# Two graph layers for 64 graphs on one core: the first weight turned in eight banks, sums two to an operation, graph 2 turned on TensorE, own orders for the last two graphs and an end in quarters

## The chip, the core and the metric

The kernel runs on one core of one Trainium2 chip, all in fp32. The metric is the device time of one execution in microseconds (us). The kernel before takes 2549.07 us, the median of three runs (2547.32 to 2550.57). The core has five engines with queues of their own: TensorE (PE) for matmuls, VectorE (DVE), ScalarE (ACT), GpSimd (POOL), and SyncE (SP), which here only issues DMA transfers. Each works its queue strictly in order, and semaphores hold an instruction until what it reads is there and what it overwrites is done with. Matmul results land in PSUM, which has eight banks of 128 x 512 fp32; everything else is in SBUF.

## The reference, cut to what matters

There are 64 graphs of 256 nodes with 512 features. `x` is 64 x 256 x 512, `adj` is 64 x 256 x 256.

```python
# layer 0
h = jnp.maximum(_layernorm(x, axis=-1), 0.0)
deg = jnp.sum(adj, axis=-1, keepdims=True)
agg = jnp.einsum('bij,bjf->bif', adj, h) / jnp.maximum(deg, EPS)
x = x + relu(jnp.einsum('bnf,of->bno', jnp.concatenate([h, agg], axis=2), W))
# layer 1
h = jnp.maximum(_layernorm(x, axis=-1), 0.0)
Xw = h @ Wv + bv
sj, si = Xw @ aw[:d, 0], Xw @ aw[d:, 0]
e = leaky_relu(sj[:, None, :] + si[:, :, None] + ab[0], 0.2)
alpha = adj * jnp.exp(e)
transition = alpha / (jnp.sum(alpha, axis=-1, keepdims=True) + 1e-12)
H, Xk = 0, h
for k in range(3):
    H = H + Xk @ Wk[k] + bk[k]
    Xk = jnp.einsum('bij,bjd->bid', transition, Xk)
x = x + relu(H)
```

## The kernel before

**The order is a table.** The kernel records every operation of the whole program in a `Plan`, with the engine it runs on, and what it reads and writes. `plan.stage(name, graph, shift)` opens a stage and sets its base, `graph * TURN + SHIFT`. Every `add(engine, cost, run, reads, writes)` in it gets the number base + `AT[stage][n]`, n counting the operations of the stage. `emit` sorts all operations by that number and hands each engine its queue in that order. The costs passed to `add` go nowhere; the numbers alone decide which operation stands before which. Graphs 0, 1 and 2 have tables of their own (`OWN = 3`, names like `wide_0`), the last four graphs have an extra `SHIFT` for each stage, and the stages `transition` and `moved` of the last two have a table `_late`.

**Start.** `first` loads x of graph 0 in two halves and the four row blocks of W0 into the buffers of x2 to x5. `weights_l0` turns W0 with 32 TensorE transposes (L725), four to a bank, in the banks 1, 2 and 0 in turn; each turned quarter of 128 x 256 is copied by ACT to SBUF (16 copies). `combine0` builds on DVE the 28 sums of quarters that the layer-0 product needs (L740, L742). `weights_l1` turns Wv (L775), forms the two score vectors v = Wv·aw on TensorE from a broadcast copy of aw (`awb`, L768; L785), puts them into `v_sb`, and forms the sums of the weights of layer 1: `lq` on DVE (L804) and `l1` on POOL (L703).

**The stages of a graph.**

- `loads`: x and adj, three graphs ahead.
- `prepare`: `norm_relu` makes h0 (L327 sum, L329 scaling of the sums on POOL, L331 squares, L333 to L335 on POOL, L337 relu), `scaled` makes adj over its row sums. Then both are turned. For graphs 0 and 1, `flip_on_pe` (L373) does it on TensorE with a copy out of PSUM (L379). From graph 2 on, `put` turns 32 x 32 blocks on DVE (L345) and stores them with four transfers from SP to DRAM (L349: `dh<-turned`, `dan<-turneda`), and `get` (L355, in the stage `prepared`) loads them back turned.
- `wide`: h0 times the wide half of W0, as a fast matrix scheme with 26 products instead of 32. 18 sums of 128 x 128 pieces of h (`LEFT_SUMS`, buffer `s`) run on POOL through `pool_op` (L389), for graph 0 on DVE (L387). Products (`P`, L426), copies from PSUM to the buffer `stg` by ACT (`S`, L438), and sums by DVE (L588) alternate in the hand-made order of `STEPS`, or of `EARLY` for graphs 0 and 1, which takes the banks 3 to 6.
- `layer0`: seven products with adj (`main`, L426, its sums at L441), and `finish` (L516), which adds relu of the bank to x.
- `turn1`: the second layernorm to h1, the scores (L613, four DVE operations with an accumulated sum), and `put` of h1.
- `transition`: the scores go to DRAM and come back as a row on all partitions (L624, L625); ACT takes exponentials (L630), DVE the larger of two and the product with adj (L633, L635), ACT the scaling (L641); then it is turned, on TensorE for the early ones.
- `moved`, `once`, `inner`, `turned1`, `outer`: the products of layer 1. `outer` ends with `main`, `finish`, and one transfer of 512 KB to the output (L694).

The engines are joined by few buffers: one `stg` of four pieces, one `p0`, one `q0`, one h0t, banks 0 to 2 for `wide` from graph 2 on and for `layer0`, banks 3 to 5 for `outer`. So the order on each engine decides how the stages of neighbouring graphs overlap.

Of the kernel before, what the change touches and what calls it, by code (L numbers as in the profile page):

```python
# [11 lines left out]
AF = mybir.ActivationFunctionType  # L12
# [13 lines left out]
TURN = 44.55  # L26
AT = {
    "first": (-1017.24, -941.27, -1067.90, -979.42, -1133.31, -1447.98, -1153.03, -1322.56, -861.36, -1000.46, -1271.51, -1112.17, -1031.96,
        -1007.46, -997.64, -1019.48, -995.91, -966.87, -807.55, -710.53, -781.12, -671.89, -691.05, -715.55, -741.64, -649.04, -668.80, -637.21,
        -513.09, -573.30, -611.16, -532.37, -616.22, -652.18, -1057.15, -794.26, -597.00, -1140.64, -889.40, -650.49, -823.54, -717.73, -1031.47,  # L30
        -761.68, -747.99, -593.69, -583.75, -527.52, -656.78, -632.97, -239.87, -431.83, -275.83, -1179.40, -946.09, -433.84, -905.70, -638.56,
        -569.10, -880.53, -782.04, -705.59, -492.83, -421.05, -288.74),
    "inner": (112.00, 118.30, 113.21, 111.00, 119.38, 119.48, 120.51, 123.95, 119.91, 117.78, 125.62, 122.20, 129.97, 123.35, 122.08, 122.94, 143.35),
    "inner_0": (120.04, 124.14, 111.34, 108.02, 121.17, 121.28, 127.27, 128.59, 125.03, 116.12, 137.98, 117.98, 127.36, 129.02, 121.84, 124.49,
        158.46),
    "inner_1": (116.30, 120.49, 114.79, 118.55, 119.44, 121.25, 125.68, 131.77, 125.03, 121.31, 129.70, 128.89, 139.17, 129.13, 123.63, 129.21,
        153.96),
    "inner_2": (117.14, 119.66, 118.60, 112.70, 119.26, 121.13, 124.83, 125.54, 119.49, 118.09, 129.51, 123.19, 123.50, 122.53, 120.98, 119.85,
        132.84),
    "layer0": (8.82, 12.23, 23.66, 30.27, 32.06, 29.03, 34.55, 32.01, 36.75, 34.14, 40.29, 34.61, 40.44, 41.44, 41.62, 36.17, 36.49),  # L40
    "layer0_0": (-200.51, -154.12, -17.22, -72.28, 8.54, -32.05, 23.63, -26.42, 30.82, -16.30, 32.72, -9.73, 34.62, 34.67, 35.87, -8.32, -3.57),
    "layer0_1": (-17.97, 4.41, -34.79, 12.11, 32.36, 15.72, 43.05, 22.64, 44.10, 24.61, 47.37, 27.04, 47.39, 47.89, 48.17, 27.25, 27.35),
    "layer0_2": (16.51, 27.98, 24.87, 29.85, 39.27, 28.73, 40.14, 29.55, 40.49, 31.62, 41.67, 35.42, 41.84, 41.86, 44.64, 35.47, 36.33),
    "loads": (-73.25, -54.78),
    "loads_2": (-570.55, -440.31),
    "moved": (96.10, 94.60, 90.90, 91.65, 92.10, 98.61),
    "moved_0": (74.40, 78.92, 73.46, 86.50),
    "moved_1": (91.74, 94.49, 96.28, 96.47, 101.59, 99.65),
    "moved_2": (92.45, 93.46, 87.17, 93.36, 88.66, 95.64),
    "moved_late": (277.68, 282.26, 301.99, 292.62),  # L50
    "once": (54.49, 60.96, 71.27, 72.69, 100.45, 102.13, 97.01, 101.40, 103.69, 104.26, 107.89, 108.15, 102.72, 101.65, 111.96, 103.21, 108.87,
        104.14, 109.67, 110.05, 110.23),
    "once_0": (61.39, 68.65, 43.72, 76.81, 102.31, 108.28, 88.12, 81.94, 109.93, 110.01, 111.86, 113.88, 100.99, 87.31, 97.51, 91.16, 118.80, 101.72,
        103.42, 103.65, 107.11),
    "once_1": (66.98, 69.71, 84.14, 73.11, 100.43, 102.58, 97.12, 100.84, 104.63, 106.78, 110.21, 112.55, 110.97, 102.83, 112.58, 108.30, 112.06,
        106.52, 108.00, 110.24, 114.90),
    "once_2": (48.31, 85.20, 76.99, 85.55, 99.90, 100.10, 96.57, 97.65, 102.25, 103.85, 102.31, 107.68, 98.75, 105.26, 111.34, 111.29, 114.34,
        108.24, 109.43, 112.02, 115.28),
    "outer": (110.55, 112.56, 124.59, 130.71, 122.70, 126.64, 130.05, 124.51, 132.31, 132.69, 134.42, 130.55, 136.29, 137.75, 137.79, 134.66, 140.16,
        142.97, 144.27, 143.30, 141.14, 144.88, 147.05, 147.31, 154.75, 166.76, 149.89, 152.90, 180.04, 173.32, 178.81, 183.03),  # L60
    "outer_0": (75.64, 100.62, 136.69, 136.53, 104.98, 130.05, 133.80, 126.65, 135.71, 136.92, 137.86, 135.82, 139.47, 140.60, 141.14, 138.11,
        143.83, 144.28, 144.84, 145.15, 143.50, 148.77, 148.79, 152.22, 164.19, 164.74, 149.82, 155.17, 176.64, 177.49, 176.45, 180.92),
    "outer_1": (116.86, 117.84, 128.53, 124.70, 122.55, 133.39, 134.11, 129.95, 135.65, 136.44, 136.94, 134.18, 139.81, 139.88, 141.12, 136.84,
        143.12, 148.89, 149.66, 146.81, 143.91, 148.56, 149.77, 153.75, 159.49, 159.72, 152.49, 156.26, 164.38, 167.52, 171.63, 187.33),
    "outer_2": (109.82, 117.34, 125.19, 132.21, 122.42, 127.44, 130.36, 123.94, 131.81, 132.14, 134.85, 131.51, 136.29, 138.25, 138.62, 135.11,
        140.08, 141.11, 142.64, 144.31, 139.88, 144.08, 146.43, 149.56, 150.02, 152.80, 151.35, 151.79, 159.27, 158.56, 152.70, 181.89),
    "prepare": (-58.85, -58.04, -62.77, -50.47, -50.61, -50.10, -47.67, -44.00, -35.79, -33.31, -40.71, -40.92, -34.53, -30.46, -9.67, -12.00,
        -30.84, -30.59, -19.83, -17.85, -13.42, -16.63, -13.01, -0.86, -2.11, 0.02, -0.84),
    "prepare_0": (-1266.53, -975.17, -811.01, -687.47, -880.33, -683.51, -631.06, -581.34, -621.45, -471.77, -1128.62, -1029.34, -1034.44, -882.61,
        -476.14, -489.14, -495.72, -471.07, -383.05, -399.08),  # L70
    "prepare_1": (-557.96, -458.29, -573.61, -253.06, -248.24, -448.75, -390.09, -379.42, -209.99, -190.33, -642.97, -325.85, -355.58, -242.70,
        -180.44, -173.98, -131.68, -163.72, -123.16, -162.03),
    "prepare_2": (-239.11, -208.13, -283.36, -178.85, -105.45, -128.88, -95.37, -80.24, -60.94, -70.06, -131.95, -63.34, -57.66, -46.88, -50.72,
        -47.06, -39.69, -38.58, -74.39, -50.57, -47.70, -74.26, -35.20, -31.13, -44.27, -36.41, -25.44),
    "prepared": (-10.65, 2.40, -0.87),
    "prepared_0": (-266.03, -448.40, -238.28, -282.28),
    "prepared_1": (-42.49, -39.69, 9.83, -23.75),
    "prepared_2": (-15.15, -0.37, 11.90),
    "transition": (55.63, 60.89, 66.16, 59.33, 66.37, 62.85, 61.19, 61.54, 61.61, 62.29, 62.78, 69.44, 69.86, 65.50, 84.98, 85.82, 78.93, 86.06),
    "transition_0": (-37.87, -34.45, 59.61, 61.95, 59.61, 59.97, 69.12, 70.02, 69.57, 70.91, 71.09, 73.37, 74.08, 94.36, 73.26, 95.01, 76.83),  # L80
    "transition_1": (41.14, 59.01, 60.68, 59.69, 61.21, 66.18, 58.69, 58.69, 58.88, 60.76, 61.81, 69.31, 69.66, 62.81, 83.27, 81.85, 79.74, 81.08),
    "transition_2": (48.98, 68.97, 59.08, 59.45, 64.06, 66.35, 59.35, 61.89, 61.81, 62.34, 62.37, 69.62, 73.39, 66.89, 81.35, 84.81, 82.67, 86.91),
    "transition_late": (-54.45, -49.51, 1.31, -11.56, 5.58, 1.28, 1.86, 18.81, 4.03, 18.88, 19.04, 24.08, 44.52, 30.73, 24.06, 60.74, 64.88),
    "turn1": (34.41, 40.31, 39.20, 37.21, 37.30, 39.30, 43.54, 44.94, 46.57, 47.03, 54.64, 55.20, 55.64, 56.82, 51.30, 51.88, 64.71, 63.98, 58.81,
        56.74),
    "turn1_0": (-37.13, -10.01, -7.88, -26.00, -25.40, -17.44, 11.38, 11.78, 24.35, 28.13, 30.44, 32.22, 43.73, 49.19, 23.26, 23.32, -152.13, -56.73,
        -93.40, -120.59),
    "turn1_1": (23.38, 31.87, 33.04, 29.38, 31.30, 34.45, 39.81, 41.29, 33.66, 34.98, 42.54, 47.50, 58.19, 58.12, 39.23, 35.62, 58.55, 66.38, 62.43,
        46.18),
    "turn1_2": (38.62, 40.24, 40.52, 41.94, 43.04, 43.41, 41.83, 46.90, 48.66, 49.26, 50.41, 54.34, 53.15, 56.69, 48.74, 51.03, 53.76, 56.22, 66.90,  # L90
        64.83),
    "turned1": (112.10,),
    "turned1_0": (76.53,),
    "turned1_1": (120.50,),
# [33 lines left out]


LEFT_SUMS = (  # L130
    (8, '-', 3, 7), (9, '+', 1, 8), (10, '+', 2, 8), (11, '-', 5, 9), (12, '-', 0, 4), (13, '-', 6, 12),
    (14, '-', 2, 13), (15, '+', 1, 3), (16, '+', 4, 6), (17, '+', 16, 15), (18, '-', 5, 12), (19, '-', 1, 18),
    (20, '+', 4, 5), (21, '+', 7, 16), (22, '+', 2, 3), (23, '+', 22, 20), (24, '+', 0, 22), (25, '-', 6, 10),
)
# [764 lines left out]
```

## Time and profile before

| | us |
|---|---|
| median of 3 runs | 2549.07 (2547.32 to 2550.57) |
| the profiled execution | 2546.46 |
| its span, first to last instruction | 2544.7 |
| TensorE busy | 2505.8 |
| VectorE busy | 1677.1 |
| ScalarE busy | 1317.8 |
| GpSimd busy | 1688.7 |
| first product of `wide` for graph 0 starts | 24.96 |
| last matmul ends | 2539.95 |

The profile gives, for one execution, the busy time of each engine, the chain of work that ended last, the groups of equal instructions with what ended the idle time ahead of them (`<-`), and the issues of the DMA queues with their time to landing. A line like `L426 PE MATMUL bank<-l,s 128x256 x3292 | 877.4, 380` names line, engine, operation, output and inputs, shape, count, busy time in us and mean ns of one. Matmuls are pipelined, so the mean of one holds its latency, and two in a row take less than twice that. These groups matter for the change:

| group | count | busy us, mean ns |
|---|---|---|
| L725 PE, transposes of W0 | 32 | 7.9, 427 |
| L775 PE, transposes of Wv | 16 | 3.4, 387 |
| L373 PE, flips of h0 | 8 | 1.7, 354 |
| L389 POOL, `s<-h0t,s`, sums of h, 128x128 | 620 | 313.2, 514 |
| L389 POOL, `s<-h0t`, sums of h, 128x128 | 372 | 199.3, 551 |
| L389 POOL, `s<-s,h1t`, sums of 128x256 | 189 | 140.9, 746 |
| L438 ACT, `stg<-bank` | 958 | 342.8, 372 |
| L329 POOL, `sm<-sm` | 128 | 29.5, 230 |
| L349 SP, `dh<-turned`, 128 KB, to landing | 504 | 3.3 us |
| L355 SP, `h0t<-dh`, 512 KB, to landing | 62 | 4.2 us |
| L694 SP, `out_dram<-x`, 512 KB, to landing | 64 | 3.1 us |

### The profile page before, as it was taken

How to read it: one execution, taken by the hardware profiler on the slowest of the kernel's cores; microseconds unless marked ns; L12 is line 12 of the kernel's file. 1: busy time of each engine (PE TensorE's matmuls, PEld its weight loads, DVE VectorE, ACT ScalarE, POOL GpSimd, SP SyncE). 2: the span in 40 equal slices, each digit the busy share in tenths (PEclk: the TensorE clock that was granted, in tenths of full speed). 3: DMA queues.
4: the chain of work that ended last, by engine and by line, in shares of the span. 5: the costliest groups of instructions: out<-in, count | busy, mean ns of one | idle time of the engine just before them, and what ended most of it. 6: DMA issues, size and time to landing. Idle time of an engine off the chain costs nothing.

```text
span 2544.7 us, 40786 instructions
## 1 busy us (share of the span) xinstructions
PE 2505.8 (98%) x12414; PEld 2211.5 (87%) x12414; DVE 1677.1 (66%) x4179; ACT 1317.8 (52%) x3490; POOL 1688.7 (66%) x3162
## 2 busy tenths in 40 slices
PE   7899999999999999999999999999999999999998
PEld 5688888888888888888888888888888888888886
DVE  5777666666666666666666666666666666666653
ACT  6555555555555555555555555555555555555521
POOL 3557766667667677667667667667666676676653
PEclk9999999999999999999999999999999999999999
DMA  4454454454454454454554554544544544545421
GB/s 137 113 128 121 114 126 118 117 128 113 115 135 113 114 127 118 119 121 115 128 121 112 128 123 112 128 119 118 125 113 119 132 112 115 133 109 121 114 67 44
DMA packets 576912, 297.95 MB, mean 117 GB/s; under 512 B 419251, under 2 KB 542899, under 8 KB 576694
## 3 DMA queue, kind: packets, MB, share of 16 engines
q1 hardware_dynamic: 576694, 295.35, 47.7%
q8 instruction: 99, 1.62, 0.3%
q14 instruction: 119, 0.97, 0.2%
HBM read 163.33 MB, written 131.92 MB: 116 GB/s over the span
## 4 chain that ended last, share of the span: by engine, by line
PE 95%; DMA 1%; DVE 1%; issue 1%; ACT 0%; POOL 0%; SPq 0%; DVEq 0%; POOLq 0%; ACTq 0%
PE bank L426 95%; DMA h0t<-dh 0%; DMA l<-in_L_gnn_Wv_dram 0%; DMA dh<-turned 0%; DMA x<-in_x_dram 0%; ACT stg L438 0%; POOL hf L389 0%; SPq L314 0%; DVE x L516 0%; POOL s L389 0%; DVE turned L345 0%; PE bank L775 0%; DVE z L613 0%; PE bank L373 0%; DVE stg L588 0%
## 5 line engine op out<-in xcount | busy, mean ns | idle before, releaser
L426 PE MATMUL bank<-l,s 128*128 128x256 f32 x3292 | 877.4, 380 | 6.8 <-DVE bank L441 2.9
L426 PEld LDWEIGHTS bank<-l,s 128*128 128x128 f32 x3292 | 609.2, 190 | 93.2 <-POOL s L389 3.9
L438 ACT COPY stg<-bank 128x256 f32<-128x256 f32 x958 | 342.8, 372 | 508.7 <-PE bank L426 188.2
L426 PE MATMUL bank<-l,zg 128*128 128x256 f32 x1820 | 468.1, 380 | 3.6 <-POOL zg L389 1.5
L426 PE MATMUL bank<-lq,zg 128*128 128x256 f32 x1792 | 448.2, 379 | 1.2 <-DVE zg L441 0.9
L426 PEld LDWEIGHTS bank<-lq,zg 128*128 128x128 f32 x1792 | 339.8, 190 | 49.5 <-DVE zg L441 1.5
L426 PEld LDWEIGHTS bank<-l,zg 128*128 128x128 f32 x1820 | 336.2, 190 | 45.7 <-POOL zg L389 1.7
L389 POOL TENSOR_TENSOR zg<-zg 128x256 f32<-128x256 f32 (+1 forms) x187 | 133.7, 728 | 355.2 <-ACT zg L438 343.3
L588 DVE TENSOR_TENSOR bank<-bank,stg 128x256 f32<-128x256 f32 x514 | 214.4, 428 | 213.5 <-PE bank L426 146.5
L389 POOL TENSOR_TENSOR s<-h0t,s 128x128 f32<-128x128 f32 x620 | 313.2, 514 | 0.0
L426 PE MATMUL bank<-l,h0t 128*128 128x256 f32 x1008 | 289.5, 380 | 2.1 <-DVE q L588 1.1
L426 PEld LDWEIGHTS bank<-l,h0t 128*128 128x128 f32 x1008 | 197.3, 196 | 25.1 <-DVE q L588 1.5
L613 DVE SCALAR_TENSOR_TENSOR z<-h1n,v_sb 128x512 f32<-128x512 f32 x256 | 200.0, 781 | 11.0 <-ACT h1n L337 2.7
L389 POOL TENSOR_TENSOR s<-h0t 128x128 f32<-128x128 f32 x372 | 199.3, 551 | 7.2 <-DMA h0t<-dh 7.2
L426 PE MATMUL bank<-l,h1t 128*128 128x256 f32 x784 | 202.1, 379 | 1.8 <-DVE lo L444 1.8
L438 ACT COPY qf<-bank 128x256 f32<-128x256 f32 x128 | 47.6, 372 | 291.1 <-DVE qf L441 258.7
L331 ACT ACTIVATE h1n<-x,sm 128x512 f32<-128x512 f32 x130 | 92.9, 715 | 158.9 <-POOL sm L329 158.9
L516 DVE SCALAR_TENSOR_TENSOR x<-bank,x 128x512 f32<-128x512 f32 x256 | 166.4, 686 | 10.4 <-PE bank L426 9.7
L426 PEld LDWEIGHTS bank<-l,h1t 128*128 128x128 f32 x784 | 152.8, 196 | 19.4 <-DVE lo L444 2.6
L329 POOL TENSOR_SCALAR sm<-sm 128x2 f32<-128x2 f32 x128 | 29.5, 230 | 197.6 <-DVE x L516 138.9
L426 PE MATMUL bank<-q,sa 128*128 128x256 f32 x512 | 153.6, 382 | 2.7 <-DVE bank L441 2.0
L389 POOL TENSOR_TENSOR qf<-qf 128x256 f32<-128x256 f32 x124 | 90.9, 733 | 98.2 <-DVE qf L441 98.2
(170 smaller groups left out, 4584.5 us busy)
## 6 DMA issues: line engine op xcount, KB each, us to landing
dh<-turned SPq DMA_DIRECT2D x504, 128.0 KB, 3.3
h1t<-dh SPq DMA_DIRECT2D x64, 512.0 KB, 3.9
out_dram<-x SPq DMA_DIRECT2D x64, 512.0 KB, 3.1
x<-in_x_dram SPq DMA_DIRECT2D x63, 512.0 KB, 4.6
h0t<-dh SPq DMA_DIRECT2D x62, 512.0 KB, 4.2
a<-in_adj_dram SPq DMA_DIRECT2D x64, 256.0 KB, 4.4
dan<-turneda SPq DMA_DIRECT2D x248, 64.0 KB, 1.9
raw<-dan SPq DMA_DIRECT2D x62, 256.0 KB, 2.7
```

Source lines behind the costliest of these rows:

```text
L329: add("POOL", 0.23, lambda: nc.gpsimd.tensor_scalar(sm, sm, -1.0 / F, None, op0=ALU.mult), [], parts(smk))
L331: add("ACT", 0.9, lambda c=c: nc.scalar.activation(h[:, c, :], s[:, c, :], AF.Square, bias=sm[:, c : c + 1], accum_out=sq[:, c : c + 1]), ...
L389: add("POOL", cost, lambda: getattr(nc.gpsimd, f)(to, p, q), reads, [write])
L426: nc.tensor.matmul(ps, lhs, rhs, start=start, stop=True, skip_group_check=True)
L438: add("ACT", 0.37, lambda: nc.scalar.copy(dst, bank[b][:, cols]), [f"bank{b}"], dkeys)
L516: add("DVE", 0.75 if sums else 0.69, lambda c=c: nc.vector.scalar_tensor_tensor(t[:, c, :], bank[banks[1 + c]], 0.0, t[:, c, :], op0=ALU.m ...
L588: add("DVE", 0.43, lambda f=f, to=to, x=x, y=y: getattr(nc.vector, f)(to, x, y), pbk + [k], tok)
L613: add("DVE", 0.83, lambda s=s, c=c: nc.vector.scalar_tensor_tensor(scr.rearrange("p c n -> p (c n)"), h[:, c, :], 1.0, v_sb[:, s, :], op0= ...
```

## The change

1. **W0.** The 32 transposes go to all eight banks in a new order. Seven of the sixteen quarters (`IN_PSUM`) are no longer copied; the DVE sums read them from PSUM. 15 of the 28 sums have such an operand. `combine0` is now part of `weights_l0`.
2. **Sums of h.** The 18 sums of `wide` are made by 9 operations of 128 x 256, two sums each (`pair` builds the access pattern with a stride between the two pieces, or a broadcast of one). `LEFT_SUMS` and `LEFT` are new. They run on POOL for graph 0 too; only its three sums in `q0` stay on DVE.
3. **Small moves.** The scaling of the sums in `norm_relu` goes from POOL to ACT. The four `lq` sums go from DVE to POOL.
4. **Graph 2.** Its h0 is turned on TensorE in the banks 0 and 1, with a copy by ACT, instead of `put` and `get`. Its scaled adj still goes through DRAM.
5. **Graph 1.** `wide(1)` uses the buffers `MZ` and half of `lo5` in place of `stg`; `layer0(1)` uses the banks 3, 4 and 5.
6. **Score vectors.** aw is used as a weight of two columns: 4 matmuls to 2 x 512 instead of 8 to 128 x 512, 4 one-column ones instead of 8, then two matmuls with `sel` (two partitions, 512 columns) and a small one spread the result to all partitions. The broadcast copy of aw is gone.
7. **The last two graphs** have tables of their own for every stage (`_late`, `_last`), and their sums in `zg`, `qf`, `st` and `hf` run on DVE.
8. **The last output.** For graph 63 `main` gets two more banks and `last`: each quarter of the result (128 x 256) is added to x by its own DVE operation and sent by its own transfer of 128 KB.
9. **All numbers** of `AT`, `SHIFT` and `TURN` (44.55 to 38.01) are new, so the order of every engine's queue changes.

```diff
-TURN = 44.55
+TURN = 38.01
...
+IN_PSUM = (27, 29, 31, 33, 35, 36, 37)
...
-        add("POOL", 0.23, lambda: nc.gpsimd.tensor_scalar(sm, sm, -1.0 / F, None, op0=ALU.mult), [], parts(smk))
+        add("ACT", 0.22, lambda: nc.scalar.mul(sm, sm, -1.0 / F), [], parts(smk))
...
     def pool_op(f, cost, to, p, q, reads, write):
-        if plan.graph < 2 and write[:2] in ("zg", "qf", "st") and plan.name[:4] != "wide" or plan.graph == 0:
+        writes = write if isinstance(write, list) else [write]
+        if plan.graph < 2 and writes[0][:2] in ("zg", "qf", "st") and plan.name[:4] != "wide" or plan.graph == 0 and writes[0][:2] == "q0" or (
+                plan.graph >= G - 2 and writes[0][:2] in ("zg", "qf", "st", "hf")):
...
-    def main(terms, banks, seeds, keys, fifth):
+    def main(terms, banks, seeds, keys, fifth, last=None):
...
+        if last:
+            x, y = banks[3:]
+            plus(bank[x][:, lo], [f"bank{x}"], p, lo, s21[:, 1], keys[1:])
+            last(1, hi, x, lo)
+            plus(bank[d][:, lo], [f"bank{d}"], p, lo, s21[:, 0], keys[:1])
+            step(2, r, lo, terms)
+            add("ACT", 0.37, lambda: nc.scalar.copy(bank[y][:, lo], bank[r][:, hi]), [f"bank{r}"], [f"bank{y}"])
+            last(0, lo, r, lo)
+            step(3, y, lo, terms)
+            last(0, hi, y, lo)
+            step(4, d, lo, terms)
+            last(1, lo, d, lo)
+            return
...
     def prepare(g):
...
+        if g < 3:
+            flip_on_pe(h, F, tr_banks if g < 2 else itertools.cycle((0, 1)), H0T[0] if g != 1 else H1T[0])
+        else:
+            put(h, F, TURNED[0], of(D["h0"], g))
         if g < 2:
             early[g] = an
-            flip_on_pe(h, F, tr_banks, H0T[0] if g == 0 else H1T[0])
         else:
-            put(h, F, TURNED[0], of(D["h0"], g))
             put(an, N, of(TURNED_A, next(turns)), of(D["an"], g))
...
-        for i, (to, op, a, b) in enumerate(LEFT_SUMS):
-            pool_op("tensor_add" if op == "+" else "tensor_sub", 0.47, sums[i][0], left[a][0], left[b][0], left[a][1] + left[b][1], sums[i][1])
-            left[to] = sums[i][0], [sums[i][1]]
+        def pair(a, b):
+
+            (x, xk), (y, yk) = left[a], left[b]
+            if a == b:
+                return x.unsqueeze(1).to_broadcast([P, 2, P]), xk
+            step = y.offset - x.offset
+            return bass.AP(tensor=x.tensor, offset=x.offset, ap=[list(x.ap[0]), [step, 2], list(x.ap[-1])]), xk + yk
+
+        for both, op, a, b in LEFT_SUMS:
+            for j in both:
+                to, key = sums(j - 8)
+                left[j] = to, [key]
+            (to, keys), (x, xk), (y, yk) = pair(*both), pair(*a), pair(*b)
+            pool_op("tensor_add" if op == "+" else "tensor_sub", 0.8, to, x, y, xk + yk, keys)
         stage = [(st[:, i], f"{stk}.{i}") for i in range(4)]
+        if g == 1:
+            stage = [(MZ[0][0][:, i], f"{MZ[0][1]}.{i}") for i in range(3)] + [(lo5[:, 1], "lo5.1")]
...
-        (p0, pk), banks = P0[0], (0, 1, 2)
+        (p0, pk), banks = P0[0], (0, 1, 2) if g != 1 else (3, 4, 5)
...
+        def last(c, cols, b, at):
+            part = t[:, c, cols], f"{k}.{c}{cols.start}"
+            add("DVE", 0.43, lambda: nc.vector.scalar_tensor_tensor(part[0], bank[b][:, at], 0.0, part[0], op0=ALU.max, op1=ALU.add),
+                [f"bank{b}", f"{k}.{c}"], [part[1]])
+            add("SP", 0.4, lambda: nc.sync.dma_start(out[g, c * P : (c + 1) * P, cols], part[0]), [part[1]], [f"out{g}.{part[1]}"], 2.2)
...
-        for n in (0, 2, 1, 3):
-            for kk in range(0, FC, 2):
-                b = next(banks)
...
+        for n, kk, b in ((0, 0, 0), (0, 2, 1), (2, 0, 6), (2, 2, 5), (1, 0, 2), (1, 2, 4), (3, 2, 3), (3, 0, 7)):
...
+                if f in IN_PSUM:
+                    assert sign > 0
+                    ps[f] = bank[b][:, cols], f"bank{b}"
...
+        def product(b=b):
+            for oc in range(FC):
+                matmul(bank[b][:2, :], awc[:, :, oc], wvt[oc][0], oc == 0)
...
         for s in range(2):
             b = next(banks)
-
-            def product(b=b, s=s):
-                for oc in range(FC):
-                    matmul(bank[b], awb[:, s, oc, :], wvt[oc][0], oc == 0)
-            add("PE", 3.45, product, awbk + [f"wvt{oc}" for oc in range(FC)] + wvt[0][1] + wvt[2][1], [f"bank{b}"])
+            add("PE", 0.9, lambda b=b, s=s: matmul(bank[b], sel[:, s], vrow[:, :F], True), vrk + ["sel"] + zk, [f"bank{b}"])
...
-            add("DVE", 0.97, lambda to=to, f=f, p=p, q=q: getattr(nc.vector, f)(WQF[to], p, q), pk + qk, [f"lq_{to}"], port=True)
+            add("POOL", 1.3, lambda to=to, f=f, p=p, q=q: getattr(nc.gpsimd, f)(WQF[to], p, q), pk + qk, [f"lq_{to}"], port=True)
...
-                kind = name + (f"_{g}" if g < OWN else "_late" if g >= G - 2 and name in ("transition", "moved") else "")
+                kind = name + (f"_{g}" if g < OWN else "_last" if g == G - 1 else "_late" if g == G - 2 else "")
```

## The prediction

> **What bounds the kernel now.** I began with the shares and the slices of the span, to see whether one engine bounds it.
>
> ```profile
> span 2544.7 us, 40786 instructions
> PE 2505.8 (98%) x12414; PEld 2211.5 (87%) x12414; DVE 1677.1 (66%) x4179; ACT 1317.8 (52%) x3490; POOL 1688.7 (66%) x3162
> PE   7899999999999999999999999999999999999998
> ```
>
> TensorE is busy 98%; only the first two slices and the last are not full. The chain of waits says how unbroken the middle is, and what held the opening.
>
> ```profile
> 75.37 5.71 DMA h0t<-dh
> ...
> 105.46 3.97 DMA h0t<-dh
> ...
> 115.86 1038.04 PE bank L426 x5172
> 1153.99 1275.86 PE bank L426 x6356
> ```
>
> From 115.86 to 2429.85 the chain is matmuls alone. So I cut the span there, and read each engine's busy time (and its instructions) by stretch; the first number after the comma is the length.
>
> ```profile
> 0.00:24.96 24.96, 12.04 (x52) 9.92 (x53) 7.53 (x23) 14.56 (x42) 4.17 (x14) 0.87 0.99 324
> 24.96:48.79 23.83, 23.62 (x106) 16.05 (x106) 16.89 (x49) 17.68 (x45) 7.72 (x10) 0.99 0.08 26
> 48.79:81.59 32.80, 24.24 (x95) 16.68 (x94) 28.18 (x73) 16.92 (x47) 17.99 (x33) 0.95 0.39 95
> 81.59:115.86 34.27, 28.24 (x135) 22.28 (x133) 26.32 (x69) 20.42 (x57) 20.58 (x44) 1.00 0.49 102
> 115.86:2429.85 2313.99, 2313.90 (x11529) 2059.24 (x11530) 1549.47 (x3852) 1222.73 (x3236) 1589.95 (x2982) 1.00 0.50 120
> 2429.85:2484.25 54.40, 53.63 (x274) 46.80 (x274) 26.45 (x64) 15.70 (x40) 29.20 (x53) 1.00 0.24 57
> 2484.25:2509.87 25.62, 22.90 (x101) 18.59 (x100) 13.80 (x34) 7.21 (x17) 10.86 (x16) 1.00 0.22 54
> 2509.87:2539.95 30.08, 27.27 (x131) 21.93 (x129) 7.60 (x17) 2.61 (x7) 8.23 (x13) 1.00 0.08 29
> ```
>
> The middle runs at 2313.99 / 11529 = 200.7 ns an instruction. Busy time overstates a starved stretch, since a matmul that follows a gap shows its whole latency; so I price each stretch by 200.7 ns times its instructions. Lost are: 12.9 us before 24.96 (24.96 − 12.04); nothing to 48.79; 32.80 − 95 × 0.2007 = 13.7; 34.27 − 135 × 0.2007 = 7.2; 110.10 − 506 × 0.2007 = 8.5 from 2429.85 to 2539.95; and 2544.70 − 2539.95 = 4.8 after the last matmul. Together 47 us. That is the ceiling of any change that leaves the matmuls as they are, and all of it lies in the first 116 us and the last 115.
>
> **Start to the first product, 12.9 us lost.** The rows that matter later stand here once:
>
> ```profile
> 21.49 2.82 PE L775 MATMUL bank<-ident,l 128*128 128x128 f32 x12 [5.11 <-DMA l<-in_L_gnn_Wv_dram]
> 24.11 1.06 PE L373 MATMUL bank<-ident,h0n 128*128 128x128 f32 x4
> ...
> 45.81 2.36 POOL L703 TENSOR_TENSOR l<-l,l 128x1024 f32<-128x1024 f32 x1
> 46.30 2.16 DVE L387 TENSOR_TENSOR q<-q 128x256 f32<-128x256 f32 x1
> ...
> 2539.50 1.29 DVE L516 SCALAR_TENSOR_TENSOR x<-bank,x 128x512 f32<-128x512 f32 x2 [4.48 <-PE bank L426]
> 2540.82 0.38 SPq L694 DMA_DIRECT2D out_dram<-x  x1
> ```
>
> Graph 0's second flip stands on TensorE behind twelve Wv transposes, which wait 5.11 us for their load. In the new order the Wv transposes stand behind both flips, among wide(0). What remains ahead is 32 W0 transposes (2.79 + 1.11 + 4.10), which still end near 14.85 since the last W0 load released them at 10.75, and two flips. The first flip needs the ACT relu that began at 14.86 (flip at 15.72); the second relu (18.18 before, behind five other ACT operations) is now next in ACT's queue, so it runs about 15.7 to 16.5, the flip to 17.1. wide(0) starts at 17.1 to 18.5; I take 17.7. TensorE's work ahead of it is 12.04 − 2.82 + 0.5 = 9.7, so 8.0 is lost. Of the 16 W0 copies (0.37 each) 7 go, their quarters being read from PSUM by 15 of the 28 sums (0.42 each, PSUM or not, as the rows `bank<-bank,stg` 428 ns and `l<-zg` 418 ns show), so ACT loses 2.6 us here.
> Against it: graph 0's 18 sums of h leave DVE (18 × 0.29 = 5.2) for POOL, in 9 pairs of 0.75 to 0.84 (rows `s<-s,h1t` 746 and `s<-h1t` 842) = 7.2 us, and matmuls wait for them one by one. I take 1.5 lost (bounds 0.5 to 5; the upper one if DVE and POOL hinder each other as at 46.30, where a sum took 2.16 beside POOL's 2.36 instead of 0.42). Loss 9.5 against 12.9: gain 3.4 (0 to 5).
> [...]
>
> **48.79 to 81.59, 13.7 lost.** Before, one chain of graph 0 goes through it: x0 done 57.12, statistics, h1n 61.97, two transposes 1.39, scores to 66.46, the store of the scores, which SP issues at 65.59, 1.6 after the first two scores (63.95), behind four h transfers, the row at 69.36, exponentials 73.27, product 77.29, `an` 78.5, flips 79.96 and 81.34, first use 84.12: 27 us. The other work that could fill it, wide(2), waits for its h0t, issued at 75.37 and 5.71 on the way. After: graph 2's h is turned on TensorE (8 × 0.11 = 0.9 us more PE work, eight DMA issues and the round trip gone), wide(1) writes its intermediate products to MZ and layer0(1) uses banks 3 to 5, so that wide(2), some 19.5 us of matmuls, can run between them. On the chain itself go 1.4 (the transposes now stand behind the first scores), that 1.6 of SP's queue (the row's two issues now precede all four h transfers), 0.4 (sm on ACT: 0.22 for POOL's 0.23, without the crossing of engines) and 1.4 (the second copy of the flips, which waited on ACT from 81.4 to 82.84): 27 to 22 us, against some 20 us of work placed ahead of its end. Loss 4 or so. **81.59 to 115.86, 7.2 lost:** its head is graph 3's h0t (issued 105.46, 3.97 in flight) and gaps at POOL's sums. The round trip stays, but pair sums cut POOL from 9.3 to 7.2 us a graph; I take 4. Together 20.9 to 8: gain 12.9. Bounds: 4, if wide(2)'s DVE and ACT hand-offs stall it as often as they stall this stretch now (nine waits, 8.5 us, over half of them behind DVE), and 17, if only the 4 us excess of the chain is left.
>
> **PE work.** The v product takes 4 matmuls of 512 columns instead of 8 (8 × 0.44 = 3.5, so 1.75 off) and 4 + 1 one-column ones instead of 8 (0.11 each, 0.35 off); two `sel` matmuls add 0.9 and the flips 0.9. Net −0.3: called 0 (−1 to 0.5). Its chain is longer by two ACT copies (0.6, 0.3); v is first needed by graph 0's scores near 62, so it is hidden; uncovered it costs 1 us.
>
> **The middle, 2314 us.** Work per graph on TensorE is the same. POOL falls by some 2 us a graph, ACT rises by 0.22 × 2, both below two thirds busy. All the queues are reordered, but TensorE works in pairs of 0.43 us and in both orders the closest hand-offs leave one pair for a DVE operation of 0.42. So nothing, the cover being TensorE's own queue. If the cover fails by 0.1 us a graph, 6 us.
>
> **The end, 8.5 + 4.8 lost.** The last tail was 1.29 of DVE (after PE) and 3.9 of SP and DMA. In quarters it is one 128x256 operation (0.43), then a 128 KB transfer: 64 KB rows (`dan`) land in 1.9 and 512 KB in 3.1, so 2.0 to 2.9. Tail 4.8 to 3.1: gain 1.7; it needs one more ACT copy (0.37), ahead of the end. Own orders for graphs 62 and 63, and DVE (0.43) for POOL (0.73) in their sums, shorten hand-offs: five at `bank L441`, 2.9 us, two at `lo L444`, 1.8. I take 8.5 to 6.9, 1.6. Gain 3.3 (0.5 to 7).
> [...]
>
> **Sum.** 3.4 + 12.9 + 0 + 0 + 3.3 = 19.6, nearly all of it at the opening. The profiled execution took 2546.46 (span 2544.7 and 1.8 around it), 2.6 below the median of 2549.07, which runs from 2547.32 to 2550.57. Against the median, 2549.07 − 19.6 = 2529.5; called 2529.
>
> **Rivals.**
> *The middle breaks* (the other side). One hand-off a graph, such as a POOL sum of a reordered queue or a scaling on ACT that now stands behind a copy, comes late. Each 0.1 us is 6 us over 60 graphs; the gain of 20 is gone at 0.33 us a graph, and from 0.42 the change is slower by 5. At 0.5 (somewhat more than one pair) it is 2529 + 30 = 2559. For it: every number of the order is new, and POOL (69%) and DVE (67%) in the middle are not idle enough to catch up at once. Against: the row of the middle has 0.09 us of idle in 2314, the work is the same or less on POOL, and distances are alike.
> *The opening stays bound.* wide(2) starts early but shares DVE with wide(1) (DVE is already 28.18 of 32.80 busy in that stretch) and the sums on POOL; what is not lost waiting for h0t is lost at DVE. Then the two stretches give 4, the start 1, the end 3.3: 2549 − 8 = 2541. For it, that 86%; against, DVE stands there behind SBUF sums that POOL stretches fivefold, as at 46.30, and the four `lq` sums (0.7 each) leave it.
> *The transfer is only swapped:* graph 3's round trip becomes the head and takes back the 4 us given to it: 2533, inside my range.
> *The change does not do what it says:* wide(2) still waits for a buffer of wide(1), and start and end alone count: 2549 − 6.7 = 2542.
>
> **How the numbers follow.** Forecast, gain of 13 to 27: 0.62. Opening bound or wide(2) still waiting, 2537 to 2544: 0.22 together. Middle broken: 0.16, half of it beyond the point where it is slower. Two executions of this kernel differ by up to 0.13%, so 0.2% (5.1 us) is about what can be told from no change. Faster 0.62 + 0.20 and 0.03 of the broken middle = 0.85, same 0.07, slower 0.08. The range goes from 2519 (bounds 5 + 17 + 7 + 1 = 30 of gain) to 2545 (a gain of 4).
>
> **What would show it.** Right: the first L426 row at 17 to 18.5; no wait for `h0t<-dh` of graph 2 and fewer than 10 us lost from 48 to the unbroken chain, which then begins about 16 us earlier for the same work; last DVE operation of 0.43 and four out transfers, the tail near 3. Wrong: gaps between 120 and 2400, which the chain would show as many short pieces behind DVE or POOL; DVE operations of 1 to 2 us beside POOL ones before 40.

## The result, and the profile after

The changed kernel takes 2596.07 us (median of 6 runs, 2594.43 to 2597.35) against 2548.38 for the kernel before (median of 6): ratio 1.0186, 95% interval 1.0173 to 1.0199. It is slower by 47.7 us, where 20 us less were forecast. The profiled execution took 2595.58, its span 2593.6.

The page of the changed kernel: span, busy engines, and the engines' shares of the chain that ended last.

```profile
span 2593.6 us, 39696 instructions
PE 2520.8 (97%) x12412; PEld 2207.0 (85%) x12412; DVE 1720.0 (66%) x4172; ACT 1325.7 (51%) x3616; POOL 1526.0 (59%) x2466
PE 59%; DMA 14%; ACT 13%; POOL 7%; DVE 5%; issue 2%; SPq 0%; POOLq 0%; DVEq 0%; ACTq 0%
```

The shares of the kernel before:

```profile
PE 95%; DMA 1%; DVE 1%; issue 1%; ACT 0%; POOL 0%; SPq 0%; DVEq 0%; POOLq 0%; ACTq 0%
```

TensorE is still busy 97%, and that one per cent says little: its share of the chain has fallen from 95% to 59%. DMA, ACT and POOL hold a third of it. The same work by stretch, cut where the unbroken chains of before have their counterparts (length after the comma, then busy time and instructions):

```profile
0.00:108.95 108.95, 82.96 (x368) 60.10 (x369) 70.44 (x172) 70.47 (x196) 61.05 (x92) 0.97 0.45 126
108.95:2400.69 2291.74, 2257.36 (x11167) 1993.48 (x11168) 1542.08 (x3734) 1193.19 (x3256) 1394.12 (x2263) 1.00 0.47 118
2400.69:2590.01 189.32, 180.50 (x878) 153.47 (x877) 107.10 (x267) 62.08 (x164) 70.82 (x113) 1.00 0.29 70
2590.01:2593.60 3.59, 0.00 (x0) 0.00 (x0) 0.42 (x1) 0.00 (x0) 0.00 (x0) 0.79 0.44 146
```

At 200.7 ns an instruction the losses are as follows, before and after. Each stretch is counted in one piece; a matmul that lies across a cut counts on both sides, so the prediction's shorter stretches add up to 388 and 506 matmuls where there are 383 and 504.

| | before | after |
|---|---|---|
| opening | 115.86 − 383 × 0.2007 = 39.0 | 108.95 − 368 × 0.2007 = 35.1 |
| middle | 0.1 | 2291.74 − 11167 × 0.2007 = 50.5 |
| end, to the last matmul | 110.10 − 504 × 0.2007 = 8.9 | 189.32 − 878 × 0.2007 = 13.1 |
| after the last matmul | 4.8 | 3.6 |

So the middle, unbroken before, loses 50 us; the opening gains 4, and the end loses some 3 net. Nearly all of TensorE's waiting in the middle has one name (total, times, longest):

```profile
PE bank L463 <- ACT tt L396: 33.9, 55, 1.2
```

Once a graph it waits 0.6 us for ACT's copy of the turned transition, `tt`; the first product of `once` reads it. With the restart that is some 0.8 a graph: in the turn shown below, the four matmuls ahead of the gap and the four behind it take 1.58 and 0.55 us from start to start, where the same eight take 0.86 and 0.44 in the kernel before. The chain of waits shows what closes on itself; here is one turn of it, the columns being start, length and what.

```profile
1231.02 22.41 PE bank L463 x116
...
1253.87 1.23 DVE x L567 x4
...
1260.63 1.51 ACT h1n L372 x2
...
1263.12 0.56 ACT ant L396
...
1263.69 5.96 DMA raw<-dtt
...
1269.67 0.66 ACT tt L396
...
1270.37 22.41 PE bank L463 x116
```

From one `once` to the next is 1270.37 − 1231.02 = 39.35 us, against the 38.5 of TensorE's own work (the turn of the first experiment below, where nothing waits). It is a ring, a chain of waits that closes on itself, so that its length sets the time of a graph: 22.41 us of matmuls end layer 0 of graph g; its x, its statistics and its relu follow; then ACT copies graph g+1's scaled adj out of `raw` to `ant`, which has nothing to do with x, but stands behind the relu in ACT's queue. Only then is the single buffer `raw` free for the load of graph g−1's transition, which takes 5.96 us, and `once` of g−1 waits for it. The kernel before has the same ring, but its load is faster. This is the load's row in the two kernels, before and after (count, size, median us to landing):

```profile
raw<-dtt SPq DMA_DIRECT2D x61, 256.0 KB, 3.0
raw<-dtt SPq DMA_DIRECT2D x61, 256.0 KB, 5.9
```

What differs around it is seen on SP's queue, first in the kernel before, then after:

```profile
1277.79 0.36 SPq L355 DMA_DIRECT2D raw<-dtt  x1
1280.11 0.34 SPq L624 DMA_DIRECT2D ds<-sj  x1
```

```profile
1263.01 0.34 SPq L692 DMA_DIRECT2D ds<-sj  x1
1263.69 0.36 SPq L390 DMA_DIRECT2D raw<-dtt  x1
```

The store of the scores (`ds`, 1 KB) used to follow the load by 2.3 us; now it goes 0.7 ahead of it. In the tables the two stand 50.84 and 50.97 (relative to graph g): 0.13 apart.

### The profile page after: what moved, and what is told of

Its sections match the earlier page's. It is cut to its first block, busy times and chain, and to the rows that moved or that the text cites. A ratio compares the mean times of both kernels' runs of the same rounds, so it can differ in the third digit from the quotient of the medians.

```text
span 2593.6 us, 39696 instructions
## 1 busy us (share of the span) xinstructions
PE 2520.8 (97%) x12412; PEld 2207.0 (85%) x12412; DVE 1720.0 (66%) x4172; ACT 1325.7 (51%) x3616; POOL 1526.0 (59%) x2466
## 4 chain that ended last, share of the span: by engine, by line
PE 59%; DMA 14%; ACT 13%; POOL 7%; DVE 5%; issue 2%; SPq 0%; POOLq 0%; DVEq 0%; ACTq 0%
PE bank L463 59%; DMA raw<-dtt 13%; ACT h1n L372 3%; ACT h1n L366 3%; POOL s L426 3%; POOL rstd L369 3%; DVE x L567 2%; ACT tt L396 1%; ACT stg L475 1%; ACT ant L396 1%; ACT an L574 1%; DVE qf L478 1%; ACT bank L649 1%; ACT sm L364 0%; POOL nmr L370 0%
## 5 line engine op out<-in xcount | busy, mean ns | idle before, releaser
L463 PE MATMUL bank<-l,s 128*128 128x256 f32 x3292 | 887.9, 380 | 4.7 <-DVE bank L478 2.5
L463 PE MATMUL bank<-lq,zg 128*128 128x256 f32 x1792 | 438.9, 380 | 4.0 <-DVE mz L478 2.9
L426 POOL TENSOR_TENSOR st<-tt 128x128 f32<-128x128 f32 x120 | 54.8, 456 | 326.2 <-ACT tt L396 326.2
L426 POOL TENSOR_TENSOR q<-q 128x256 f32<-128x256 f32 x189 | 166.8, 895 | 117.6 <-DVE q L656 117.6
L426 POOL TENSOR_TENSOR s<-h0t,s 128x256 f32<-128x256 f32 x315 | 230.9, 741 | 0.7
L364 ACT ACTIVATE sm<-sm 128x2 f32<-128x2 f32 x128 | 26.1, 204 | 333.6 <-DVE x L567 331.7
L681 DVE SCALAR_TENSOR_TENSOR z<-h1n,v_sb 128x512 f32<-128x512 f32 x256 | 177.3, 692 | 20.3 <-ACT h1n L372 13.6
L426 POOL TENSOR_TENSOR zg<-zg 128x256 f32<-128x256 f32 x180 | 141.0, 783 | 79.2 <-DVE zg L478 59.5
L426 POOL TENSOR_TENSOR sa<-ant 128x128 f32<-128x128 f32 x128 | 59.2, 462 | 183.6 <-ACT ant L396 183.6
L426 POOL TENSOR_TENSOR s<-h0t 128x256 f32<-128x256 f32 x189 | 143.4, 772 | 19.3 <-ACT h0t L414 8.9
```

The costliest lines, as they stand in the source:

```text
L364: add("ACT", 0.22, lambda: nc.scalar.mul(sm, sm, -1.0 / F), [], parts(smk))
L426: add("POOL", cost, lambda: getattr(nc.gpsimd, f)(to, p, q), reads, writes)
L463: nc.tensor.matmul(ps, lhs, rhs, start=start, stop=True, skip_group_check=True)
L681: add("DVE", 0.79, lambda s=s, c=c: nc.vector.scalar_tensor_tensor(scr.rearrange("p c n -> p (c n)"), h[:, c, :], 1.0, v_sb[:, s, :], op0= ...
```

## The experiments

All edits are to the changed kernel unless said otherwise. The numbers of the tables are relative to a graph's base, and where an edit holds for some graphs only, the new numbers stand in a table of their own for these.

**The ring cut at both strands.** For graphs 5 to 57 the copy to `ant` goes ahead of the relu, the load ahead of the store.

```diff
-    "prepared": (-13.22, 3.34, 8.63),
+    "prepared": (-13.22, 3.34, 4.49),
-    "moved": (88.98, 92.24, ...),
+    "moved": (87.51, 92.24, ...),
```

> Theory (a ring): graph g's x leads through its relu on ACT to the copy of `raw` to `ant`, which stands behind that relu; only then is `raw` free for the load of `dtt`, and the first product of `once` waits for that. With the copy ahead of the relu, and the load ahead of the scores' store on SP, for graphs 5 to 57, the ring is cut: the first product of `once` no longer waits, a graph takes 38.5 us instead of 39.4, and the time falls by about 53 x 0.83 = 44 us, to some 2552. Rival (the queues as a whole are too tight): the wait moves to another hand-off of DVE, POOL or ACT, and less than half of the 44 us comes back: above 2574.

Measured 2550.47 (before beside it 2548.01): 45.6 us less. The load lands in 2.7, and the chain is matmuls alone from 243.16 to 2279.9:

```profile
243.16 2036.74 PE bank L465 x10148
```

In that stretch the wait moved nowhere else. (Whether a second buffer for `raw` would do the same was not tried.)

**Only the copy to `ant`.**

> Only the copy of `raw` to `ant` goes ahead of the relu; the load of `dtt` still stands behind the store of the scores on SP, which issues at 1263.01 where the load issued at 1263.69. Theory (a ring, with two strands of nearly one length): the load moves by 0.3 us only, so some 53 x 0.33 = 17 us come back, about 2579. If the copy alone were the cause, all 44 would come back (2552); if it had no part, nothing (2596).

Measured 2587.87: 8.2 us less, half of what was expected, and far from 44. The load still goes 0.43 behind the store and lands in 6.1.

**Only the load ahead of the store.**

> Only the load of `dtt` goes ahead of the store of the scores on SP. Theory: it still waits for the copy at 1263.67, so nothing comes back (2596); the store of the scores is 0.7 us later, which costs nothing if the row has room. If SP's queue alone were the cause, 44 us would come back (2552).

Measured 2556.84 (one run): 39 us less, where nothing was expected. My theory of two strands of one length was wrong. The load is still issued when the copy behind the relu frees the buffer, 0.4 us ahead of the store; but its median landing is 2.8, and that alone makes the ring shorter than TensorE's work. TensorE waits for `tt` 8 times instead of 55. So the copy behind the relu is a part of the ring, but not what made it too long. The order has a price for the other side: the store, now 0.4 us behind the load, lands in a median of 5.2 us (3.8 in the changed kernel, 3.0 in the first experiment).

**What else is in flight moved away.** For graphs 5 to 57 the first h1 store and the load of x, issued 2 us behind the slow load, go behind the row.

```diff
-    "turn1": (..., 58.21, 56.06, 54.36, 57.84),
-    "loads": (-58.38, -36.44),
+    "turn1": (..., 58.21, 56.06, 56.00, 57.84),
+    "loads": (-50.00, -36.44),
```

> The order of raw, `ant` and the scores stays; the first of the four h1 stores and the load of x, which SP issues 2 us behind the load of `dtt`, go behind the row. Theory of a collision of transfers: the load of `dtt` then takes about 3 us, as in the kernel before, instead of 5.9; the ring is then 39.4 - 2.9 = 36.5 us, shorter than the 38.5 of TensorE's work, and about 44 us come back (2552) though nothing else is changed. If the 5.9 us have another cause, the landing time stays and so does the time (2596).

Measured 2654.53: 58 us slower. As a test of the time it missed, since the edit made a ring of its own: x, behind stores that wait, now comes just when graph g+3's statistics need it (the chain has 9.8% of `x<-in_x_dram`). But the landing answers the question: 5.4 us, with x 18 us and the h1 store 3.3 us behind the load, when a load of 3 us would have landed. So these two were not what made it slow.

**The store moved away instead.** The scores' store goes behind the first h1 store and x; the load keeps its place and its neighbours.

```diff
-    "transition": (50.84, 55.74, ...),
+    "transition": (55.70, 55.74, ...),
```

> In the changed kernel the store of the scores (1 KB) moves behind the first h1 store and the load of x on SP, for graphs 5 to 57; `ant` and the load of `dtt` keep their places, so that load is still issued when the copy behind the relu frees `raw`. Theory (the load of `dtt` is slow since it is issued 0.4 to 0.7 us behind the store of the scores): it lands in about 2.8 us instead of 5.9 with the h1 store and x still behind it, the ring is 39.4 - 3.0 = 36.4 us, and the time falls to some 2552. Rival (it is slow by sharing with the h1 store and x): the landing stays near 5.9 and the time near 2596. If both count, in between.

Measured 2641.66, again a miss in time for a reason of its own: the scores, their row and the softmax are late, and the chain now has 15% of `ds<-sj` in a window of 60 us (9% over the whole execution). The landing is 2.7, with the h1 store 2.1 and x 2.5 us behind the load, as before the edit. Together the two runs settle it: the load is slow with the store close ahead of it, and not by the bigger transfers behind it.

**The kernel before, with the load put behind the store.** One number changed, for graphs 5 to 57.

```diff
-    "moved": (96.10, 94.60, ...),
+    "moved": (100.20, 94.60, ...),
```

> The kernel before with one number changed: for graphs 5 to 57 the load of `dtt` goes right behind the store of the scores on SP, as in the changed kernel. In its profile the load is issued at 1277.79 and lands in 3.0, the store is issued at 1280.11, and between the copy `tt` and the first product of `once` there are 2.2 us of slack. Theory (the load is slow behind the store, and the ring counts here too): the load is issued 2.7 us later and lands in 5.9, 5.6 us late in all, 3.4 past the slack, with 0.3 for the restart of TensorE: 53 x 3.7 = 196 us, about 2745; the landing time of `raw<-dtt` becomes about 5.9. If the landing stays at 3.0: 0.5 past the slack, 53 x 0.8 = 42 us, about 2590. If there is no ring through this load: 2548.

Measured 2804.58: 257 us slower, by a change of one place in one queue. The landing is 6.1, and TensorE waits for `tt` 53 times, 179.7 us in all, 3.4 each as worked out. That and the restarts make the expected 196; the other 61 go with the clock. In these rows of its busy times by stretch the number after POOL's is TensorE's granted clock, for the end of the work, the wait, and three times behind it:

```profile
1321.00:1326.00 5.00, 5.00 (x25) 4.26 (x23) 4.17 (x11) 1.83 (x7) 1.69 (x3) 1.00 0.21 63
1326.00:1330.00 4.00, 0.33 (x2) 0.15 (x2) 1.42 (x6) 0.84 (x2) 0.12 (x1) 1.00 0.94 213
1330.00:1332.00 2.00, 2.00 (x11) 1.84 (x12) 0.00 (x0) 1.35 (x4) 1.92 (x5) 0.78 0.77 204
1332.00:1334.00 2.00, 2.00 (x8) 1.64 (x7) 0.00 (x0) 0.17 (x1) 2.00 (x5) 0.50 0.02 4
1334.00:1336.00 2.00, 2.00 (x12) 1.78 (x11) 0.69 (x2) 0.22 (x1) 2.00 (x6) 0.86 0.00 0
```

Behind this wait of 3.67 us the clock is at a half for 3.4 us, as worked out from these rows (0.88 + 2.00 + 0.56). Its mean over the execution is 0.976 against 0.998: 0.022 × 2803 = 62 us as an estimate, which closes the sum (196 + 62 = 258); at 3.4 / 2 = 1.7 us each, that would be 36 of the 53 waits. With the waits of 0.6 us in the changed kernel the mean stays at 0.998.

**The ring cut for all graphs** (graphs 3 to 61 for the copy, 3 to 60 for the load).

> The cut of the ring as before, now for graphs 3 to 61 (the copy) and 3 to 60 (the load). Theory: the three waits at graphs 3 to 5 that are left (about 0.8 us each) go: 2 to 3 us below 2550.5, so 2548, equal to the kernel before within 0.2%.

Measured 2548.97, ratio to the kernel before 1.0006 (0.9998 to 1.0015). Against the kernel before beside it, the first cut was 2.5 us above and this one is 1.9: 0.6 came back of the 2 to 3 expected. With every part of the change in it and two numbers of the order mended, the kernel is as fast as before. What the change lost, the order lost.

**Two places of the opening mended**, on top of that: POOL's l1 sum away from DVE's softmax product, and DVE's transposes of graph 3 behind two sums that `inner` waits for.

```diff
-    "weights": (..., 84.67, 94.37, ...),
+    "weights": (..., 81.70, 94.37, ...),
-    "prepare" of graph 3: (..., 97.99, 97.94, ...)
+    "prepare" of graph 3: (..., 98.90, 98.87, ...)
```

> As the run with the ring cut for all graphs, and two places of the opening mended: one of POOL's l1 sums (2.5 us) goes ahead, to where POOL stood idle for 2.4 us, away from DVE's product of graph 0's scores with adj (2.56 us beside it, 0.42 alone); and DVE's transposes of graph 3's h0 go behind two sums that the first products of `inner` wait for. Theory (the opening's loss sits in single hand-offs, of which these are the longest, 2.2 and 1.3 us of wait): 3 to 4 us less than the run with the ring cut alone, about 2544. Rival (the gain is given back at the next hand-off, since DVE and POOL are what bounds the opening): less than 1 us.

Measured 2546.33, ratio to the kernel before 1.0000 (0.9991 to 1.0009), 2.6 under the run it is built on, with overlapping ranges (2545.64 to 2550.68, and 2546.6 to 2551.98). In the profiles the unbroken chain begins 1.5 us earlier, at 176.09 for 177.62; the 2.2 us wait of the changed kernel behind the softmax product did not occur in the profile of the run that this one is built on, so it tells little of that place. Of the other wait, 1.5, more than all came back as one of 2.62 a few us later. This is its row:

```profile
102.08 0.87 PE L466 MATMUL bank<-l,s 128*128 128x256 f32 x2 [2.62 <-DVE stg L659]
```

**Graph 0's sums of h on DVE**, as before the change, with the ring cut.

```diff
-... or plan.graph == 0 and writes[0][:2] == "q0" or (
+... or plan.graph == 0 and writes[0][:2] in ("q0", "s0") or (
```

> As the run with the ring cut for all graphs, but graph 0's nine pair sums of h run on DVE at the same places of the order, not on POOL. The prediction took 1.5 us as the cost of their move to POOL (0.5 to 5). If POOL is what holds the first product stage: up to 3 us faster. If DVE, with the 28 W0 sums, is the tighter of the two: slower, by up to 9 x 0.42 = 4 us.

Measured 2549.92, 1.0 above the run with the ring cut, ranges overlapping; the unbroken chain begins 1.9 us later (179.47 for 177.62). So the move to POOL shows no cost, where the prediction had 1.5; a gain of 1 is not told apart from none.

**All of it, and the next two waits**: two sums of graph 2 go ahead of the softmax products on DVE (102.45 and 102.92 to 99.60 and 99.70), and at the end a sum and a finish go behind the copy of the last `tt`.

> All parts of the change with the ring cut for all graphs, the two places of the opening mended, two sums of graph 2 put ahead of graph 1's softmax products on DVE (2.6 us of wait there), and at the end DVE's copy of the last turned transition ahead of a sum and a finish that wait longer (0.9 us). Theory (what is left of the loss are single hand-offs): 2.6 + 0.9 and two restarts, some 3 to 4 us less than the run with the opening mended, about 2543, which would be faster than the kernel before by 0.15%. Rival (given back at the next hand-off): 2546.

Measured 2545.76, ratio to the kernel before 0.9992 (0.9983 to 1.0001): the best of all, 50 us under the changed kernel, and not told apart from the kernel before. It is the rival's 2546, not the theory's 2543. The wait of 2.62 is gone and this one stands in its place:

```profile
102.81 1.13 PE L459 MATMUL bank<-lq,zg 128*128 128x256 f32 x4 [2.45 <-ACT qf L471]
```

## Why the prediction was wrong, point by point

**The middle: the step that failed.** The prediction costed it at nothing, "the cover being TensorE's own queue", because the closest hand-offs of DVE looked alike in both orders. That looked at one hand-off at a time. What broke is a ring through DVE, POOL, ACT, SP and a transfer, closed by one single buffer. In the kernel before it had 2.2 us of slack (`tt` copied at 1281.03 + 0.66 = 1281.69, first read at 1283.88); the new order made one transfer on it 3 us longer.

```profile
1281.03 0.66 ACT L361 COPY tt<-raw 128x512 f32<-128x512 f32 x1
...
1283.88 0.61 PE L426 MATMUL bank<-tt,h1n 128*128 128x128 f32 x4
```

The sum had no term for the transition's way through DRAM at all. Its measured size is 50.5 us.

**The rival "the middle breaks"** had the right kind of event (one late hand-off a graph) and the right law: at its 0.1 us a graph for 6 us, the 0.84 per turn give 50. Its place was wrong (a POOL sum or an ACT scaling, not a load), its example of 0.5 too small, and with a chance of 0.16 it was not what the forecast went by. The prediction's sign of being wrong, gaps between 120 and 2400, was there, behind a transfer and ACT more than behind DVE or POOL.

**The opening, 16.3 us of gain forecast (3.4 and 12.9), 4 found.** The first product of `wide` came at 18.89 (17.1 to 18.5 forecast, 24.96 before), behind the second flip, which waited 2.33 us for ACT's copy of the first, and the sums of h went to POOL without harm. But up to 48.79 the loss fell only from 48.79 − 157 × 0.2007 = 17.3 to 48.79 − 164 × 0.2007 = 15.9. The prediction's 12.9 there was too low by its own price: it took busy time ahead of 24.96 and nothing behind it, where 24.96 − 52 × 0.2007 = 14.5 and 23.83 − 106 × 0.2007 = 2.6. And the stretch behind the first product has waits of its own now: TensorE is idle there for 29.90 − 28.48 = 1.4 us, 0.2 before. The two stretches from 48.79 to the end of the opening were the step that failed: they lose 32.80 − 116 × 0.2007 = 9.5 and 27.36 − 90 × 0.2007 = 9.3, not 8 together. The upstream gain was real. Graph 0's x was done 4.6 us earlier (52.6 for 57.2), and the row went out 8.4 us earlier (60.91 for 69.36). Then it was given back: the four exponentials, 1.78 in one piece before, were spread from 67.00 to 70.10 between other ACT work; the maximum began at 72.10 behind layer 0 of graph 1; and the products ran beside a POOL sum. These are DVE and POOL in the changed kernel:

```profile
74.01 2.53 POOL L781 TENSOR_TENSOR l<-l,l 128x1024 f32<-128x1024 f32 x1
...
74.27 2.55 DVE L703 SCALAR_TENSOR_TENSOR z<-z,a 128x256 f32<-128x256 f32 x1
```

The second product took 2.55 instead of 0.42, and the flips came at 77.83 against 79.96. That is the rival "the opening stays bound": it gave the opening 5 us of gain, and 4 were found. The mended versions agree: each wait taken away there came back for the most part at the next engine. Which engine bounds the opening as a whole was not settled.

**The end, 3.3 forecast.** The tail was right: 3.59 after the last matmul instead of 4.75, a gain of 1.2 against 1.7, the last operation at 0.42, and the 128 KB transfers landing in 1.8, under the 2.0 to 2.9 of the sum. The gaps were wrong: 13.1 lost instead of 6.9. That stretch begins earlier than the one before the change and holds one last wait of the ring, but this is not the reason: in the run with the ring cut for all graphs the end still loses 160.26 − 732 × 0.2007 = 13.3, against 8.9 before. With their own orders for the last two graphs there are more waits, not fewer (from 2380 us on, 16 for 10, together 8.3 us for 5.9; in the run with the ring cut, one of 1.03 behind exponentials on ACT and the softmax on DVE that follows them, and one of 0.87 behind two operations on DVE, are new). It was not tried apart from the rest.

**PE work**, called 0: the count of instructions is the same to two.

DVE operations were stretched beside POOL sums of weights as above, and once ahead of 40, where a DVE sum took 2.31 us at 34.93 beside a POOL one of 2.35 from 34.19; but graph 0's sums of h, where the prediction had feared it, showed no cost (2548.97 with them on POOL, 2549.92 on DVE). Why the load of `dtt` is slow behind the small store, 5.4 to 6.1 us against 2.7, no run here shows. The trace adds that it is not the signal alone that comes late. In the changed kernel the DMA engines moved 0.13 MB from 1263.6 to 1266.6, no more than half of the load (0.26 MB); in the kernel before they moved 0.79 MB from 1277.8 to 1281.1, which is the whole load and the output of 512 KB issued 0.9 us ahead of it.

## What to carry to other kernels

Where every engine's order is written by hand, list the rings: from a buffer's release through each queue back to its next use, transfers with their landing times. The shortest slack of a ring, not the nearest pair of operations, says whether a new order is safe. Ask of each transfer on a ring what goes out just ahead of it on the same queue, and put a load that others wait for ahead of a small store, if the store can bear to land later (here the load landed in 2.8 us for 5.9, the store in 5.2 for 3.8). A busy share of 97% can hide a loss of 2% (here 50.5 of 2596 us): the chain's share by engine shows it at once (59% for 95%).

## What the runs showed of the hardware that had not been expected

- The load of `dtt`, 256 KB, landed in a median of 2.7 to 3.0 us where the store of 1 KB of scores went out behind it (four runs), though in the kernel before an output of 512 KB goes out 0.9 us ahead of it; it landed in 5.4 to 6.1 where the store went out 0.4 to 0.7 us ahead (four runs and two kernels). With the store 0.4 us behind it, where the median was 2.8, one load at 1242.28 took 6.08.
- 53 waits of TensorE, once a graph, of 3.4 us in the mean and 3.8 at the longest (the kernel before with the load behind the store), came with a mean granted clock of 0.976 for 0.998; behind one of 3.67 us it was at a half for 3.4 us. By the estimate above the lower clock cost some 62 us beside the 180 of the waits themselves, and came behind 36 of the 53; on what it depends no run here shows. With 55 waits of 0.6 us (the changed kernel) the mean clock was 0.998.
